# The spacer of the weight stage: first product of V of a later pair in place of the first product of scores and v

## The chip, the cores and the metric

The kernel runs on one core of a Trainium2 chip. The metric is the device time of one execution in microseconds (us). Before the change it is 1761.79 us, the median of three runs (1760.82 to 1763.11). One execution was also recorded by the hardware profiler; its span, from the first to the last instruction, is 1759.4 us. The engines go by these names: PE is TensorE (matrix products), PEld its weight loads, DVE is VectorE, ACT is ScalarE, POOL is GpSimd, SP is SyncE. A "q" behind a name is the engine's instruction queue.

## The reference, cut to what matters

`x` has 64 samples of 256 tokens and 512 features in fp32, `adj` is 256 x 256, and the weights are 512 x 512. Two layers follow each other:

```python
# layer 0
h = relu(layernorm(x))
q, k, v = h @ Wq.T, h @ Wk.T, h @ Wv.T
rel = adj.T * (q @ k.T)
rel = rel / norm(rel, axis=2)          # one norm for each row
x = x + rel @ v
# layer 1
h = relu(layernorm(x))
x = x + (adj @ h) @ weight + bias
```

The samples do not depend on each other. Nothing but the order of the work is at stake here: the change computes the same numbers with the same operations.

## The kernel before, in words

The kernel takes two samples at a time, a **pair**; there are 32 pairs (`NP`). For each pair it computes, in this order: layer norm 0 and its transpose `ht`; `g`, which is `h` times the product of the two weights Wq and Wk, made once at the start (`project_g`, L264); `V = h Wv` (`v_products`, L276); the scores `rel` from `g` and `h` (`scores`, L288), which are then masked, normed, and transposed by blocks (16 small transfers, `placed`, and four transposes on DVE, `turns`, L546); the product of scores and v, added to `x` (called **attend** here, `attend_steps`, L612, adds in L619); layer norm 1; the gather with `adj` (`gather_steps`, L675); and the **weight stage** `mix`, which multiplies by `weight` and adds to `x` (L276 again, adds in L703). Then the pair is written out.

Each of these large products is done by a scheme of Winograd's kind: the operands are cut in 2 x 2 blocks, seven block products take the place of eight, and DVE makes sums of blocks ahead of them. The seven steps use the PSUM tiles `bank_a`, `bank_c`, `bank_b`; after a step, a `take` copies (ACT) or adds (DVE) the tile to its place, while PE goes on with the next. In `project_g`, V and `mix` one of the seven, step 2, is cut once more in the same way ("two levels"): its seven small products go to a tile `bank_d` in four groups, and DVE adds them in small operations (L449, L491). `two_level_steps` (L234) puts the groups between the six large products, which it calls `one`, `five`, `six`, `three`, `seven`, `four`. The last group needs that DVE has already added the third one, so a `spacer`, a product from another part of the work, may be put in front of it:

```python
lambda: run([seven, groups[2]]),
lambda: run([spacer, groups[3]] if spacer else [groups[3]]),
lambda: run([four]),
```

The order of instructions on PE, DVE and ACT is written out by hand: each engine runs its instructions as the program lists them. No planner moves them. The dictionaries in the calls (`{0: ..., 1: ...}`, called `side`) hang DVE and ACT work behind the steps of a product: slot 3 is what is listed after the fourth step and its take. The waits between engines, and which of the eight PSUM buffers a tile gets, are set by the framework.

`steady(i)` (L894) works on several pairs at once, and runs for i = 1 to 28. Its stages are:

1. attend of pair i, interleaved step by step with V of pair i+1 (`attend_and_v`, L623). In its side slots: layer norm 0 of pair i+3 (`totals`, `mean`, `row_squares`, ... on ACT and DVE), the sums for the scores (`gs`), and the last operands of attend itself (`late`)
2. scores of pair i+1
3. `project_g` of pair i+2, with the first part of the gather of pair i as its spacer
4. the rest of the gather of pair i
5. `mix` of pair i. Its spacer is `attends[0]`, the first product of attend of pair i+1. The next pass then leaves this product out (`first_done`)

The operands of attend of pair i+1 are prepared by DVE: `v_steps` make four sums of blocks of V (L133 to L136), `turns` transpose the scores (slot 4 of `mix`), and `rel_steps` make four sums of those (L168 to L171). The first attend product needs the first transposes and a block of V alone; the second needs `v_steps[1]` and `rel_steps[1]`, the third `v_steps[2]` and `rel_steps[2]`. `last_pairs` (L935) finishes the three last pairs.

Of the kernel before, what the change touches and what calls it, by code (L numbers as in the profile page):

```python
# [19 lines left out]
def kernel(  # L20
# [65 lines left out]
    def load(i, queue=nc.sync):  # L86
        X[i] = ring[i % len(ring)]
        queue.dma_start(out=X[i], in_=xs[i])
# [64 lines left out]
    def run(steps):  # L153
        for step in steps:
            step()
# [78 lines left out]
    def two_level_steps(product, take, matmul, add, spacer):  # L234

        one, five, six, three, seven, _, four = winograd_steps(product, take)
        groups = second_level(matmul, add)
        return [  # L240
            lambda: run([one]),
            lambda: run([five]),
            lambda: run([six, groups[0]]),
            lambda: run([three, groups[1]]),
# [4 lines that stand above are left out]
# [125 lines left out]
    def ln0_by_scalar(i):  # L374
        H[i] = work.tile([P, TC, D], F32, tag="hy", name=f"h_{i}")
        return norm_by_scalar(flat(X[i]), H[i])
# [91 lines left out]
    def v_products(i):  # L468
        V[i] = twice.tile([P, NB, NC, D], F32, tag="v", name=f"v_{i}")

        def take(t, k, bank, first):
            dst = V[i][:, :, t, k * HD : (k + 1) * HD]
            src = bank.rearrange("p (b e) -> p b e", b=NB)
            if first:
                nc.scalar.copy(dst, src)  # L475
            else:
                nc.vector.tensor_add(dst, src, dst)

        return product_weights_moving(HL[i], wv_right), take

    def project_v(i, side={}):
        winograd(*v_products(i), side)

    def second_weights_moving(left, right, x):

        def matmul(out, n, start):
            nc.tensor.matmul(out, left[n], right[n], start=start, stop=True, skip_group_check=True)  # L487

        def add(b, k, sums):
            dst = x[:, b, 0, 0:HD] if k is None else x[:, b, 0, ts(k, P)]  # L490
            nc.vector.tensor_add(dst, sums, dst)  # L491

        return matmul, add

    def v_steps_by_two_levels(i):
        products = v_products(i)
        second = second_weights_moving(HL2.pop(i), wv_second, V[i])
        return two_level_steps(*products, *second, None)
# [107 lines left out]
    def attend_steps(i):  # L606

        xt, (left, right) = X[i], R.pop(i)

        def product(bank, n, start):  # L610
            for b in range(NB):
                nc.tensor.matmul(  # L612
                    bank[:, ts(b, HD)], left[n][:, b], right[n][:, b],
                    start=(start and b == 0), stop=True, skip_group_check=True,
                )

        def take(t, k, bank, first):
            dst = xt[:, :, t, ts(k, HD)]
            nc.vector.tensor_add(dst, bank.rearrange("p (b e) -> p b e", b=NB), dst)  # L619

        return winograd_steps(product, take)

    def attend_and_v(i, first_done, steps, side):  # L623


        for at, (step, v_step) in enumerate(zip(steps, v_steps_by_two_levels(i + 1))):
            if at or not first_done:
                step()
            v_step()
            run(side.get(at, ()))  # L630


# [188 lines left out]
    def pairs(exact):  # L821
        with tc.manual_schedule(engines=in_order):
            sums = first_pairs(exact)
            attends, late = attend_steps(1), []
            for i in range(1, NP - 3):
                if i + 4 < NP:
                    load(i + 4)
                sums, attends, late = steady(i, exact, sums, attends, late, first_done=i > 1)
            last_pairs(exact, sums, attends, late)

    def first_pairs(exact):

# [58 lines left out]
        })  # L891
        return sums3

    def steady(i, exact, sums, attends, late, first_done):  # L894

        gs = g_operands(i + 1)
        totals, mean, row_squares, root0, end0, relus0 = ln0_by_scalar(i + 3)  # L900
        stats, root, end, relus, uppers, lowers = ln1(i, exact)
        halves = [stats[b * NC + t] for t in range(NC) for b in range(NB)]
        attend_and_v(i, first_done, attends, {
            0: late[0:3] + totals[0:2], 1: late[3:4] + totals[2:4] + [mean] + sums[0:1],
            2: row_squares[0:2] + sums[1:3], 3: row_squares[2:4] + [root0, end0] + sums[3:4],
            4: relus0[0:2] + gs[0:1], 5: relus0[2:4] + gs[1:3], 6: gs[3:4] + halves[0:1],
        })
        place_blocks(i + 3)
        h_second = second_of_h(i + 2)
        masks, squares, norm_root, inverse, scales, place, turns = scores(i + 1, {  # L910
            0: halves[1:2], 1: halves[2:3], 2: halves[3:4], 3: [root], 4: [end] + relus[0:1],
            5: relus[1:2], 6: uppers[0:2] + h_second,
        })
        turned, sums = transpose_blocks(i + 3)
        y_products, y_steps = gather_steps(i, exact)
        project_g(i + 2, {
            0: masks[0:1] + lowers[0:1] + relus[2:3],
            1: masks[1:2] + lowers[1:2] + relus[3:4],
            2: uppers[2:4] + squares[0:2] + turned[0:2],
            3: lowers[2:3] + squares[2:4] + [norm_root] + turned[2:4],  # L920
            4: lowers[3:4] + [inverse] + scales + [place] + turned[4:5],
            5: turned[5:8],
        }, second=True, spacer=y_products[0])
        v_steps, rel_steps = attend_operands(i + 1)
        run_steps(y_products[1:], {0: v_steps[0:1], 1: v_steps[1:2]})
        run(y_steps[0:2])
        y_second = second_of_y(i)
        attends = attend_steps(i + 1)
        mix(i, {
            0: y_steps[2:3], 1: y_steps[3:4] + y_second[0:2], 2: y_second[2:4],  # L930
            4: turns, 5: rel_steps[0:2],
        }, spacer=attends[0])
        return sums, attends, v_steps[2:3] + rel_steps[2:4] + v_steps[3:4]

    def last_pairs(exact, sums, attends, late):  # L935

        a, b, c = NP - 3, NP - 2, NP - 1
        gs = g_operands(b)
        stats, root, end, relus, uppers, lowers = ln1(a, exact)
        halves = [stats[e * NC + t] for t in range(NC) for e in range(NB)]  # L940
        run(late)
        attend_and_v(a, True, attends, {
            1: sums[0:1], 2: gs[0:2], 3: gs[2:3], 4: gs[3:4], 5: sums[1:2], 6: halves[0:2],
        })
        masks, squares, norm_root, inverse, scales, place, turns = scores(b, {
            0: halves[2:3], 1: halves[3:4] + [root], 2: [end], 3: relus[0:1],
            4: relus[1:2], 5: uppers[0:1], 6: uppers[1:2] + sums[2:4],
        })
        project_g(c, {
            0: masks[0:1] + lowers[0:1] + relus[2:3],  # L950
            1: masks[1:2] + lowers[1:2] + relus[3:4],
            2: uppers[2:4] + squares[0:2],
            3: lowers[2:3] + squares[2:4] + [norm_root],
            4: lowers[3:4] + [inverse] + scales + [place],
        })
        y_steps = gather(a, exact)
        gs = g_operands(c, spare_blocks())
        project_v(c, {
            0: gs[0:1], 1: gs[1:2], 2: gs[2:3] + y_steps[0:1], 3: gs[3:4], 4: y_steps[1:2],
            5: y_steps[2:4], 6: turns,  # L960
        })
        masks, squares, norm_root, inverse, rn, turn_at_once = scores(c, by_matmul=True)
        stats, *parts = ln1(b, exact)
        attend(b, by_slot({n: [stats[n]] for n in range(TC)}, {
            1: masks[0:1], 2: masks[1:2] + squares[0:2], 3: squares[2:4],
        }))
        mix(a, by_slot({0: [norm_root, inverse]}, layer_1(parts)))
        turn_at_once()
        y_steps = gather(b, exact)
        stats, *parts = ln1(c, exact)  # L970
        attend(c, {0: [stats[0], y_steps[0]], 1: [stats[1], y_steps[1]], 2: [stats[2]], 3: [stats[3]]}, rn)
        mix(b, by_slot({0: y_steps[2:3], 1: y_steps[3:4]}, layer_1(parts)))
        y_steps = gather(c, exact)
        run(y_steps[0:2])
        mix(c, {0: y_steps[2:4]})
# [36 lines left out]
```

## Time and profile before

The profile's page gives each engine's busy time and its share of the span; each group of instructions has a row with its busy time, the mean of one instruction, and how long the engine stood idle just before it. The rows for the stages around the change:

| what | line, engine | mean of one | count in all |
|---|---|---|---|
| V product, matmuls (and those of `mix`) | L276 PE | 379 ns | 8 records to a product |
| attend product, matmuls | L612 PE | 379 to 397 ns | 4 records to a product |
| small products of V and `mix` | L487 PE | 274 to 291 ns | 2 records to a product |
| copy of a V product | L475 ACT | 586 ns | 96 from `bank_a` |
| add of a `mix` product | L703 DVE | 691 ns | 128 from `bank_a`, 64 from `bank_c` |
| add of an attend product | L619 DVE | 685 ns | 116 from `bank_a` |
| transposes of scores | L546 DVE | 411 ns | 124 |
| small adds to V and `x` | L491 DVE | 281, 283 ns | 145, 140 of 128 columns |
| sums of V blocks | L133 to L136 DVE | 682 to 692 ns | 29 each |

Matmuls overlap, so the mean of one is longer than the distance from one to the next. In the timeline a row merges equal instructions that follow each other; the distance between the starts of two rows tells what the first of them takes from PE when nothing waits.

Three terms are of use. The **chain of waits** follows the run back from its last instruction, at each step to what released it. A **releaser** is the instruction that an engine was waiting for when it stood idle. A **slot** is a place in a side dictionary.

### The profile page before, as it was taken

What the parts mean: (1) busy time and instruction counts of PE and PEld (TensorE: products, weight loads), DVE (VectorE), ACT (ScalarE), POOL (GpSimd) and SP (SyncE); (2) the same over time, 40 slices, a digit from 0 to 9 for tenths busy, and PEclk for the clock granted to TensorE, in tenths of its full rate; (3) what the DMA queues carried; (4) which work ended last, traced back from release to release, by engine and by line L of the source; (5) the groups of instructions that cost most, each with busy time, mean ns of one, the idle gap of its engine ahead of it and who ended that gap; (6) DMA issues with size and microseconds to landing.
All of it is one profiled execution on the core that took longest, in us unless ns stands there. A gap on an engine that the chain in (4) does not pass through costs nothing.

```text
span 1759.4 us, 27004 instructions
## 1 busy us (share of the span) xinstructions
PE 1711.0 (97%) x9680; PEld 1525.2 (87%) x9680; DVE 1393.6 (79%) x3141; ACT 791.4 (45%) x1835; POOL 192.2 (11%) x167
## 2 busy tenths in 40 slices
PE   9999999999999999999999999999999999999998
PEld 7888988889888898888898888988888988889886
DVE  6778887788877888877888778887778888788765
ACT  3434544445444355444454344554444544445332
POOL 0011110111101111001111011110011110111111
PEclk9999999999999999999999999999999999999999
DMA  7423332323332333323233322333233332322002
GB/s 233 66 50 61 76 81 68 75 38 79 78 76 69 57 64 74 83 65 61 56 78 79 74 71 41 79 74 83 63 60 61 76 81 69 75 37 57 28 13 75
DMA packets 425984, 122.48 MB, mean 70 GB/s; under 512 B 398064, under 2 KB 399344, under 8 KB 425840
## 3 DMA queue, kind: packets, MB, share of 16 engines
q1 hardware_dynamic: 413248, 80.28, 24.4%
q0 software_dynamic: 8432, 32.51, 4.9%
q10 hardware_dynamic: 4160, 7.87, 1.3%
q8 instruction: 79, 1.29, 0.3%
q14 instruction: 65, 0.53, 0.1%
HBM read 38.27 MB, written 33.55 MB: 41 GB/s over the span
## 4 chain that ended last, share of the span: by engine, by line
PE 92%; DVE 4%; SPq 1%; issue 1%; DMA 1%; ACT 0%; DVEq 0%; ACTq 0%
PE bank_a L276 24%; PE bank_c L276 12%; PE bank_a L264 12%; PE py L675 7%; PE bank_a L288 6%; PE bank_c L264 6%; PE bank_a L612 6%; PE bank_d L487 5%; PE bank_c L288 3%; PE bank_c L612 3%; PE bank_d L440 3%; PE bank_b L288 2%; PE bank_b L612 1%; DVE x_ring L703 1%; DVE x_ring L491 1%
## 5 line engine op out<-in xcount | busy, mean ns | idle before, releaser
L475 ACT COPY v<-bank_a 128x512 f32<-128x512 f32 x96 | 56.2, 586 | 582.5 <-PE bank_a L276 582.5
L647 POOL TENSOR_TENSOR x_ring<-x_ring,bias_bc 128x512 f32<-128x512 f32 x128 | 167.4, 1327 | 841.9 <-ACT h2c L319 841.9
L703 DVE TENSOR_TENSOR x_ring<-bank_a,x_ring 128x512 f32<-128x512 f32 x128 | 88.4, 691 | 61.9 <-PE bank_a L276 61.9
L675 PE MATMUL py<-adjt_r,h 128*128 128x256 f32 x1024 | 136.5, 287 | 0.0
L319 ACT ACTIVATE h2c<-x_ring,nb,rs 128x512 f32<-128x512 f32 x128 | 100.6, 810 | 63.8 <-DVE h L655 45.1
L675 PEld LDWEIGHTS py<-adjt_r,h 128*128 128x128 f32 x1024 | 125.3, 189 | 1.6
L276 PE MATMUL bank_a<-w_t,ys 128*128 128x256 f32 x512 | 121.1, 379 | 0.3 <-DVE ys L170 0.3
L264 PE MATMUL bank_a<-hs,m_t 128*128 128x256 f32 x512 | 121.0, 379 | 0.0
L276 PE MATMUL bank_a<-wv_t,hs 128*128 128x256 f32 x512 | 120.9, 379 | 0.0
L276 PEld LDWEIGHTS bank_a<-wv_t,hs 128*128 128x128 f32 x512 | 97.3, 190 | 13.2
L276 PEld LDWEIGHTS bank_a<-w_t,ys 128*128 128x128 f32 x512 | 92.9, 190 | 14.6 <-DVE ys L170 0.7
L264 PEld LDWEIGHTS bank_a<-hs,m_t 128*128 128x128 f32 x512 | 95.1, 190 | 11.8
L715 POOL DMA_DIRECT2D out_dram<-x_ring x31 | 24.0, 773 | 705.2 <-issue 515.3
L307 DVE BATCH_NORM_STATS2 st<-x_ring 128x6 f32<-128x512 f32 x144 | 96.4, 670 | 0.4
L416 DVE STREAM_TRANSPOSE ht<-blocks 128x256 f32<-128x256 f32 x248 | 93.5, 417 | 3.6 <-DMA blocks<-h 3.3
L655 DVE TENSOR_TENSOR h<-h2c,h 128x512 fp32r<-128x512 f32 x128 | 92.3, 723 | 3.0 <-ACT h L651 2.9
L354 ACT ACTIVATE h<-x_ring,nb,rs 128x512 f32<-128x512 f32 x112 | 82.0, 803 | 12.4 <-DVE nb L351 12.4
L619 DVE TENSOR_TENSOR x_ring<-bank_a,x_ring 128x512 f32<-128x512 f32 x116 | 79.5, 685 | 9.9 <-PE bank_a L612 9.9
L679 ACT COPY yt<-py 128x512 f32<-128x512 f32 x128 | 74.4, 581 | 25.6 <-PE py L675 25.6
L536 ACT ACTIVATE rel<-rel,rn 128x256 f32<-128x256 f32 x124 | 52.9, 497 | 68.5 <-DVE rn L533 68.5
L340 ACT ACTIVATE h<-x_ring,sm 128x512 f32<-128x512 f32 x112 | 79.5, 714 | 0.0
L651 ACT CAST h<-h2c 128x512 fp32r<-128x512 f32 x128 | 72.8, 616 | 0.0
(229 smaller groups left out, 4105.0 us busy)
## 6 DMA issues: line engine op xcount, KB each, us to landing
blocks<-h SPq DMA_DIRECT2D x496, 64.0 KB, 2.3
out_dram<-x_ring POOLq DMA_DIRECT2D x31, 1024.0 KB, 4.7
x_ring<-in_x_dram SPq DMA_DIRECT2D x28, 1024.0 KB, 5.2
placed<-rel SPq DMA_DIRECT2D x496, 32.0 KB, 2.0
x_ring<-in_x_dram ACTq DMA_DIRECT2D x4, 1024.0 KB, 5.4
wq_sb<-in_L_gnn_Wq_dram SPq DMA_DIRECT2D x4, 256.0 KB, 5.1
wk_sb<-in_L_gnn_Wk_dram ACTq DMA_DIRECT2D x4, 256.0 KB, 6.2
wv_sb<-in_L_gnn_Wv_dram ACTq DMA_DIRECT2D x1, 1024.0 KB, 5.2
```

The lines of the kernel that those rows point to most:

```text
L264: nc.tensor.matmul(bank[:, e * HT_ : (e + 1) * HT_], right[n][:, d, ts(e, P)], left[n][:, d, :], start=(start and e == 0 and d == 0), stop ...
L276: nc.tensor.matmul(bank[:, b * HD : (b + 1) * HD], left[n][:, d, ts(b, P)], right[n][:, d, :], start=(start and b == 0 and d == 0), stop=( ...
L288: nc.tensor.matmul(bank[:, ts(b, P)], right[n][:, d, ts(b, P)], left[n][:, d, ts(b, P)], start=(start and b == 0 and d == 0), stop=(d == H ...
L307: nc.vector.bn_stats(st[:, c, :], src[:, c, :])
L319: nc.scalar.activation(dst, src[:, c, :], AF.Relu, bias=nb[:, c : c + 1], scale=rs[:, c : c + 1])
L416: nc.vector.transpose(ht[:, d, half].rearrange("p (b n) -> p b n", b=NB), by_half[:, :, half, d])
L487: nc.tensor.matmul(out, left[n], right[n], start=start, stop=True, skip_group_check=True)
L612: nc.tensor.matmul(bank[:, ts(b, HD)], left[n][:, b], right[n][:, b], start=(start and b == 0), stop=True, skip_group_check=True,)
L647: nc.gpsimd.tensor_tensor(xt[:, c, :], xt[:, c, :], bias_bc, ALU.add)
L655: nc.vector.tensor_sub(dst[:, 1, c, :], whole_h[c], dst[:, 0, c, :].bitcast(F32))
L675: nc.tensor.matmul(pm[:, d, :], left[:, b * NC + m, ts(d0 + d, P)], right, start=(n == 0), stop=(n == len(terms) - 1),)
L703: nc.vector.tensor_add(xt[block], bank.rearrange("p (b e) -> p b e", b=NB), xt[block])
```

## The change

The spacer of `mix` becomes the first V product of pair i+2; the first attend product of pair i+1 goes back to the attend stage, directly behind the weight stage. Hence the attend stage now begins with its own first step, and leaves out the first step of V. As the last operands of attend are needed a little earlier now, they are no longer made in the attend stage (`late`), but in slots 3 and 6 of `mix`. The freed side slots of the attend stage are evened out. The purpose is that the spacer should be work whose operands are long there.

```diff
-    def attend_and_v(i, first_done, steps, side):
-        for at, (step, v_step) in enumerate(zip(steps, v_steps_by_two_levels(i + 1))):
+    def attend_and_v(i, first_done, v_products, side):
+        for at, (step, v_step) in enumerate(zip(attend_steps(i), v_products)):
+            step()
             if at or not first_done:
-                step()
-            v_step()
+                v_step()
             run(side.get(at, ()))
...
-            attends, late = attend_steps(1), []
+            v_products = v_steps_by_two_levels(2)
...
-    def steady(i, exact, sums, attends, late, first_done):
+    def steady(i, exact, sums, v_products, first_done):
...
-        attend_and_v(i, first_done, attends, {
-            0: late[0:3] + totals[0:2], 1: late[3:4] + totals[2:4] + [mean] + sums[0:1],
-            2: row_squares[0:2] + sums[1:3], 3: row_squares[2:4] + [root0, end0] + sums[3:4],
+        attend_and_v(i, first_done, v_products, {
+            0: totals[0:2] + sums[0:1], 1: totals[2:4] + [mean] + sums[1:2],
+            2: row_squares[0:2] + sums[2:3], 3: row_squares[2:4] + [root0, end0] + sums[3:4],
             4: relus0[0:2] + gs[0:1], 5: relus0[2:4] + gs[1:3], 6: gs[3:4] + halves[0:1],
         })
...
-        attends = attend_steps(i + 1)
+        v_products = v_steps_by_two_levels(i + 2)
         mix(i, {
             0: y_steps[2:3], 1: y_steps[3:4] + y_second[0:2], 2: y_second[2:4],
-            4: turns, 5: rel_steps[0:2],
-        }, spacer=attends[0])
-        return sums, attends, v_steps[2:3] + rel_steps[2:4] + v_steps[3:4]
+            3: v_steps[2:4], 4: turns, 5: rel_steps[0:2], 6: rel_steps[2:4],
+        }, spacer=v_products[0])
+        return sums, v_products
...
-    def last_pairs(exact, sums, attends, late):
+    def last_pairs(exact, sums, v_products):
...
-        run(late)
-        attend_and_v(a, True, attends, {
+        attend_and_v(a, True, v_products, {
```

More of the change, by code (lines that the diff above doesn't have):

```diff
@@ L827, in pairs @@
                     load(i + 4)
-                sums, attends, late = steady(i, exact, sums, attends, late, first_done=i > 1)
-            last_pairs(exact, sums, attends, late)
+                sums, v_products = steady(i, exact, sums, v_products, first_done=i > 1)
+            last_pairs(exact, sums, v_products)
     def first_pairs(exact):
```

## The prediction

> **What bounds the kernel now.** First the page: which engine is full, and at what clock.
>
> ```profile
> span 1759.4 us, 27004 instructions
> PE 1711.0 (97%) x9680; PEld 1525.2 (87%) x9680; DVE 1393.6 (79%) x3141; ACT 791.4 (45%) x1835; POOL 192.2 (11%) x167
> ...
> PEclk9999999999999999999999999999999999999999
> ```
>
> TensorE has work almost always, at full clock (the mean granted clock is 0.999), and the chain that ended last runs 92% over it. So only two things can shorten the run: less TensorE work, or fewer TensorE waits. The list of waits of PE names one that repeats; the other matmul waits of the whole run are under 6 us together.
>
> ```profile
> PE bank_a L612 <- DVE turned L546: 36.8, 28, 1.4
> ```
>
> 28 waits, one for each `steady` pair, 36.8/28 = 1.31 us each and 1.4 at most: every pair loses the same. The timeline of PE around one of them (columns: start, length, engine, line, operation, count, idle before it):
>
> ```profile
> 820.23 1.89 PE L276 MATMUL bank_a<-w_t,ys 128*128 128x256 f32 x8
> 821.96 0.38 PE L487 MATMUL bank_d<-w_t,ys 128*128 128x128 f32 x2
> 822.18 0.39 PE L487 MATMUL bank_d<-w_sb,yt 128*128 128x128 f32 x2
> 823.88 1.10 PE L612 MATMUL bank_a<-v,turned 128*128 128x256 f32 x4 [1.31 <-DVE turned L546]
> 824.82 0.39 PE L487 MATMUL bank_d<-w_t,yt 128*128 128x128 f32 x2
> 825.04 1.89 PE L276 MATMUL bank_a<-w_t,yt 128*128 128x256 f32 x8
> 826.77 1.89 PE L276 MATMUL bank_a<-wvt_sb,ht 128*128 128x256 f32 x8
> 828.50 1.03 PE L612 MATMUL bank_c<-v,turned 128*128 128x256 f32 x4
> 829.36 1.89 PE L276 MATMUL bank_c<-wvt_sb,ht 128*128 128x256 f32 x8
> ```
>
> Read it by starts. A full product of weights or V takes 1.73 (825.04 to 826.77), an attend product 0.86 (828.50 to 829.36), a pair of 128-wide matmuls 0.22 (821.96 to 822.18). After the third row PE could go on at 822.18 + 0.22 = 822.40. The spacer, the first product of scores and v (`attends[0]`, L612), starts at 823.88: 1.48 late. It then takes 0.94 to the next start in place of 0.86. The loss is 1.48 + 0.08 = **1.56 us per pair**, of which the wait shows 1.31, since the printed ends lie later than the point at which the next matmul could start. What it waited for is in DVE's timeline:
>
> ```profile
> 819.99 0.69 DVE L703 TENSOR_TENSOR x_ring<-bank_c,x_ring 128x512 f32<-128x512 f32 x1 [0.72 <-PE bank_c L276]
> 820.60 0.28 DVE L491 TENSOR_TENSOR x_ring<-bank_d,x_ring 128x128 f32<-128x128 f32 x1
> 822.16 0.69 DVE L703 TENSOR_TENSOR x_ring<-bank_a,x_ring 128x512 f32<-128x512 f32 x1 [1.28 <-PE bank_a L276]
> 822.77 0.61 DVE L491 TENSOR_TENSOR x_ring<-bank_d,x_ring 128x128 f32<-128x128 f32 x2
> 823.30 1.41 DVE L546 STREAM_TRANSPOSE turned<-placed 128x256 f32<-128x256 f32 x4
> ```
>
> DVE idles 1.28 until the fifth big product (`seven`) ends, adds it, adds the two small sums, and only then transposes the scores (`turns`, L546). The spacer needs the first of these transposes. Thus a product meant to fill a pause waits for the very queue that made the pause.
>
> **What the Trainium skill says.** "Perfetto Trace Analysis", section "Tensor Engine Instruction (MATMUL, LD_WEIGHTS)": ends of matmuls are estimated from their size. The trace agrees: rows of 1.89 follow each other every 1.73; hence my counting by starts. "TensorE: Matmul & The Clock Gate", "Step-by-step: what each phase is for": matmuls stay in program order, only weight loads are pulled ahead. The trace agrees: `group_4` (824.82) and `four` (825.04) need no transpose and still stand behind the spacer. "PSUM — Partial Sum Buffer", "Specifications (TRN2)": 8 banks of 512 fp32 values; each `bank_*` or `py` tile fills one. No row of the trace shows which bank a tile has, so this feeds a rival.
>
> **The change, part by part.**
>
> 1. *Spacer.* `attends[0]` leaves the slot, `v_products[0]` of pair i+2 enters: 8 matmuls, 1.73 us in all. Its operands are `ht` and `wvt_sb`. `project_g(i+2)` has already read this `ht` over 10 us before, so it waits for no operand. Work between 822.40 and the later V product is the same set in another order, so no PE work is added: 0.
>
> 2. *The new order on PE*, from 822.40 with the steps above: V product to 824.13, `group_4` to 824.35, `four` to 826.08, attend product 1 to 826.94, attend product 2 to 827.81, then V product 2, which before started at 829.36. 829.36 - 827.81 = 1.55, if nothing waits.
>
> 3. *DVE's queue.* `v_steps[2:4]` come from the attend stage to slot 3 (L135 and L136, 0.68 each, starts 0.6 apart). They enter behind the L491 of 820.60 and end at about 822.2, where DVE had idled to 822.16: cost 0 to 0.15. Then the add of `seven` to 822.9, two small adds to 823.4, four transposes to 824.75, the add of `group_4` to 825.05, `rel_steps[0:2]` (0.42 each) to 825.9, the add of `four` at 826.2 to 826.9, `rel_steps[2:4]` to 827.7, the add of attend product 1 to 828.4.
>
> 4. *What PE needs from it.* `group_4` at 824.13 needs the small adds (823.4): 0.7 to spare. Attend product 1 at 826.08 needs the transposes (824.75): 1.3. Product 2 at 826.94 needs `rel_steps[1]` and `v_steps[1]` (825.9): 1.0. Product 3 at 829.54 needs the add of product 1 (828.4): 1.1. None waits; the thinnest is 0.7, before `group_4`.
>
> 5. *ACT.* The V product is taken by an ACT copy (L475, 0.58) in the weight stage. In this pair ACT had idled 16.01 us ahead of that very copy: 0.
>
> 6. *Attend and V stage.* It loses four DVE operations (2 x 0.68 + 2 x 0.42 = 2.2 us) and 1.73 of PE, and gains one attend product (0.86 PE, 0.69 DVE): DVE has less to do there. `totals[2:4]` still stand behind the second V copy and `mean` behind them, so they keep their distance to PE. The transfers that place the blocks start at the end of the last attend product, in the same order as before: 0. Work of `scores`, `project_g` and the gather is untouched.
>
> 7. *Ends.* The first pass has no spacer behind it in either order, and `last_pairs` takes the spacer of the last of the 28 passes. The wait that vanishes occurs 28 times.
>
> Sum: 28 x 1.55 = 43.4; 1761.8 - 43.4 = **1718.4 us**, some 2.5% less. The lower bound of the gain from the waits alone is 36.8 (1725.0).
>
> **Rivals.**
>
> *A, the wait reappears smaller.* DVE is the other busy engine (43.7 busy of 54.0 us of a pair). If its queue is 1.1 us later than I draw it, `group_4` or an attend product waits 0.4 us: 28 x 0.4 = 11.2, **1729.6**. For it: two more operations of 0.68 in front of the transposes. Against: DVE idled 1.28 exactly there, and the only other regular wait of TensorE for DVE, that of V's own `group_4` (weight loads for L491: 11.3 us, 28 times), is 0.4 and has no V product in front of it, only an attend product of 0.86.
>
> *B, a PSUM bank comes late at the start of the weight stage.* The spacer's set of tiles, asked for before `mix`, has four banks now against three, `mix` has four: all eight. If `mix`'s first product gets the bank of the last gather tile, it waits for that tile's ACT copy, which ends at 812.69, where the product now starts at 811.91: 0.8 per pair, 22.4, **1740.8**. Against: eleven tiles over the three sets share eight banks in either order, and the trace has no PE wait of this kind.
>
> *C, slower.* If also attend product 1 gets the bank of `four`, it waits until DVE has added it. The add of `four` started at 826.97 and ended 0.69 later, 0.9 after that product's last matmul had given way (826.77). 0.8 + 0.9 = 1.7 of new waits against 1.55 saved: 28 x 0.15 = +4, **1766**. For: attend tiles are now first used directly behind `four`. Against: the V tiles stood in that place before and started at once at 826.77.
>
> **How the numbers follow.** The forecast has 0.71 (1716 to 1722: the loss is the same in every pair, and the saving is 1.48 to 1.63 according to how the starts are rounded). A and smaller mixtures have 0.17 (1722 to 1737), B 0.05, no net change 0.02, C 0.05. Below 1716 I leave 0.02, from the forecast's share. The range 1716 to 1731 holds 0.69 of the forecast and some 0.11 of A, so 0.8. Faster: 0.71 + 0.17 + 0.05 = 0.93; within 0.2%: 0.02; slower: 0.05.
>
> **What would show it.** Right: no wait of PE for `turned`; the V product (bank_a from `wvt_sb`, `ht`) starts 0.22 after the last L487 of the third group; L612 rows for bank_a and bank_c stand one behind the other after `four`; the spacing of pairs falls from 53.94 (823.88 to 877.82) to 52.4; PE at about 99% of its span. A shows as a wait of L487 for L491, or of L612 for L169 or L619; B as a wait of L276 (`yt`) for the copy L679; C as a wait of the first L612 for L703. The prediction is wrong if one of these is over 0.15 us per pair, or if DVE's `mean` (L337) falls later against PE and pushes adds into the V groups.

## The result, and the profile after

The changed kernel takes **1718.93 us** (median of 4 runs, 1717.26 to 1719.96), against 1762.22 us for the kernel before in the runs beside it. The ratio is 0.9754, with a 95% interval of 0.9737 to 0.9771: 43.3 us less. The prediction said 1718.4.

The page of the kernel after, its first lines and the granted clock:

```profile
span 1715.2 us, 27061 instructions
PE 1704.2 (99%) x9680; PEld 1523.6 (89%) x9680; DVE 1386.5 (81%) x3141; ACT 794.5 (46%) x1835; POOL 192.2 (11%) x167
...
PEclk9999999999999999999999999999999999999999
```

The number of PE instructions and the clock are the same; the span fell by 44.2, while PE's busy time fell by 7 only. So what went was idle time, and the 7 us were no work either: per pair the loss read by starts (1.56) exceeds the printed wait (1.31) by 0.25, and 28 x 0.25 = 7.0. Of this 0.25, 0.17 is the printed end of the row ahead of the wait (822.18 + 0.39 = 822.57), which lies later than the point at which PE could go on (822.40), and 0.08 is the slower start after the wait. PE's list of waits in the kernel after (line, releaser, total, count, longest) begins so:

```profile
PE pf L758 <- DVE low_max L756: 1.3, 1, 1.3
PE pz L743 <- POOL warm L105: 1.0, 1, 1.0
PE bank_a L276 <- DMA wk_sb<-in_L_gnn_Wk_dram: 1.0, 1, 1.0
```

The row of 28 waits for `turned` is gone. What is left at the head belongs to the start of the run, each once. PE's timeline at the place of the change, kernel after:

```profile
802.50 0.39 PE L487 MATMUL bank_d<-w_sb,yt 128*128 128x128 f32 x2
802.73 1.89 PE L276 MATMUL bank_a<-wvt_sb,ht 128*128 128x256 f32 x8
804.45 0.39 PE L487 MATMUL bank_d<-w_t,yt 128*128 128x128 f32 x2
804.67 1.89 PE L276 MATMUL bank_a<-w_t,yt 128*128 128x256 f32 x8
806.40 1.03 PE L612 MATMUL bank_a<-v,turned 128*128 128x256 f32 x4
807.27 1.03 PE L612 MATMUL bank_c<-v,turned 128*128 128x256 f32 x4
808.13 1.89 PE L276 MATMUL bank_c<-wvt_sb,ht 128*128 128x256 f32 x8
809.86 1.03 PE L612 MATMUL bank_a<-blocks,rel 128*128 128x256 f32 x4
```

No row carries an idle time. From the moment PE is free after the third group (802.73) to the second V product (808.13) it takes 5.40 us; before it was 829.36 - 822.40 = 6.96. The difference is 1.56, the loss that was read off the trace of before. DVE's timeline of the same stretch, kernel after:

```profile
800.92 0.28 DVE L491 TENSOR_TENSOR x_ring<-bank_d,x_ring 128x128 f32<-128x128 f32 x1
801.11 0.68 DVE L135 TENSOR_TENSOR blocks<-v 128x512 f32<-128x512 f32 x1
801.83 0.69 DVE L136 TENSOR_TENSOR blocks<-v,blocks 128x512 f32<-128x512 f32 x1
802.48 0.69 DVE L703 TENSOR_TENSOR x_ring<-bank_a,x_ring 128x512 f32<-128x512 f32 x1
803.09 0.61 DVE L491 TENSOR_TENSOR x_ring<-bank_d,x_ring 128x128 f32<-128x128 f32 x2
803.62 1.42 DVE L546 STREAM_TRANSPOSE turned<-placed 128x256 f32<-128x256 f32 x4
804.96 0.25 DVE L491 TENSOR_TENSOR x_ring<-bank_d,x_ring 128x128 f32<-128x128 f32 x1
805.13 0.41 DVE L168 TENSOR_TENSOR rel<-turned 128x256 f32<-128x256 f32 x1
805.57 0.43 DVE L169 TENSOR_TENSOR turned<-turned 128x256 f32<-128x256 f32 x1
```

The two moved sums (L135, L136) fill the pause of 1.28 us that stood in front of L703 before. DVE does the transposes no earlier against PE than before: 1.12 us after the start of the last L487 row (803.62 - 802.50; before 823.30 - 822.18). Only nobody waits for them now; their reader starts at 806.40.

### The profile page after: what moved, and what is told of

The parts are those of the page before. It is cut to its first block, busy times and chain, and to the rows that moved or that the text cites. A ratio compares the mean times of both kernels' runs of the same rounds, so it can differ in the third digit from the quotient of the medians.

```text
span 1715.2 us, 27061 instructions
## 1 busy us (share of the span) xinstructions
PE 1704.2 (99%) x9680; PEld 1523.6 (89%) x9680; DVE 1386.5 (81%) x3141; ACT 794.5 (46%) x1835; POOL 192.2 (11%) x167
## 4 chain that ended last, share of the span: by engine, by line
PE 97%; DVE 2%; DMA 0%; ACT 0%; issue 0%; ACTq 0%; DVEq 0%
PE bank_a L276 26%; PE bank_c L276 13%; PE bank_a L264 13%; PE py L675 7%; PE bank_a L288 7%; PE bank_c L264 6%; PE bank_d L487 6%; PE bank_a L612 6%; PE bank_c L288 3%; PE bank_c L612 3%; PE bank_d L440 3%; PE bank_b L288 2%; PE bank_b L612 1%; PE bank_b L276 1%; PE pu L577 1%; DVE st L307 0%
## 5 line engine op out<-in xcount | busy, mean ns | idle before, releaser
L276 PE MATMUL bank_a<-w_t,ys 128*128 128x256 f32 x512 | 121.1, 379 | 0.3 <-DVE ys L170 0.3
L276 PE MATMUL bank_a<-wv_t,hs 128*128 128x256 f32 x512 | 120.9, 379 | 0.0
L703 DVE TENSOR_TENSOR x_ring<-bank_a,x_ring 128x512 f32<-128x512 f32 x128 | 88.5, 691 | 35.1 <-PE bank_a L276 35.1
L276 PEld LDWEIGHTS bank_a<-wv_t,hs 128*128 128x128 f32 x512 | 97.3, 190 | 13.2
L276 PEld LDWEIGHTS bank_a<-w_t,ys 128*128 128x128 f32 x512 | 92.9, 190 | 14.6 <-DVE ys L170 0.7
L264 PEld LDWEIGHTS bank_a<-hs,m_t 128*128 128x128 f32 x512 | 95.1, 190 | 11.8
L334 ACT ACTIVATE h<-x_ring 128x512 f32<-128x512 f32 x112 | 69.5, 623 | 40.5 <-PE bank_a L276 40.5
L679 ACT COPY yt<-py 128x512 f32<-128x512 f32 x128 | 74.5, 582 | 26.1 <-PE py L675 26.1
L619 DVE TENSOR_TENSOR x_ring<-bank_a,x_ring 128x512 f32<-128x512 f32 x116 | 79.3, 683 | 1.0 <-PE bank_a L612 1.0
```

The costliest lines, as they stand in the source:

```text
L264: nc.tensor.matmul(bank[:, e * HT_ : (e + 1) * HT_], right[n][:, d, ts(e, P)], left[n][:, d, :], start=(start and e == 0 and d == 0), stop ...
L276: nc.tensor.matmul(bank[:, b * HD : (b + 1) * HD], left[n][:, d, ts(b, P)], right[n][:, d, :], start=(start and b == 0 and d == 0), stop=( ...
L703: nc.vector.tensor_add(xt[block], bank.rearrange("p (b e) -> p b e", b=NB), xt[block])
```

## The experiments

In what follows, group 3 and group 4 are the last two of the four groups of small products. Two theories were told apart first. **Theory 1**: the gain is the wait of the spacer for the transposes. **Theory 2**: it is the better spread of DVE's work over the slots, which the change also contains.

**The slots alone.** The kernel before, with the side slots of the kernel after (those of the attend stage too, which the cut leaves out):

```diff
...
-            4: turns, 5: rel_steps[0:2],
+            3: v_steps[2:4], 4: turns, 5: rel_steps[0:2], 6: rel_steps[2:4],
         }, spacer=attends[0])
-        return sums, attends, v_steps[2:3] + rel_steps[2:4] + v_steps[3:4]
+        return sums, attends, []
```

> The kernel before with the side slots of the kernel after (no late operands, v_steps[2:4] and rel_steps[2:4] in mix), but with the first attend product still as the spacer. Theory 1 (the gain is the spacer's wait for the transposes that vanished): the wait stays, and the transposes come 0 to 0.15 us later behind the two moved sums: 1762 to 1766 us, a wait of L612 for turned of 1.3 to 1.5 us, 28 times. Theory 2 (the gain comes from DVE's work being spread better): about 1719 us.

Measured: 1761.87 us, ratio to before 1.0001 (0.9992 to 1.0009). PE's waits in this run:

```profile
PE bank_a L612 <- DVE turned L546: 36.7, 28, 1.4
```

The wait is as long as before (36.8), and the time did not move. Theory 2 falls.

**The spacer alone.** The kernel after, with the late operands where they were before:

```diff
...
-            3: v_steps[2:4], 4: turns, 5: rel_steps[0:2], 6: rel_steps[2:4],
+            4: turns, 5: rel_steps[0:2],
         }, spacer=v_products[0])
-        return sums, v_products
+        return sums, v_products, v_steps[2:3] + rel_steps[2:4] + v_steps[3:4]
```

> The kernel after with the late operands kept in the attend stage, in the slots of the kernel before; the spacer is the V product. Theory 1: 1717 to 1723 us; the third attend product needs rel_steps[2], which would end some 0.5 us before that product can start, so no wait of TensorE, or one below 0.15 us per pair (4 us). Theory 2: about 1762 us. A third reading (the moved slots are needed so that the new order does not wait for its own operands): the third attend product waits for L170 or L171 by 0.3 us or more per pair, 1727 us or more.

Measured: 1718.91 us, ratio 0.9755 (0.9739 to 0.9771). It is the whole gain. So the spacer's place is what counts, and moving the four DVE operations, which the change does as well, is not needed for it.

**No spacer at all.** Is it enough that nothing waits for the transposes, or must a product cover DVE's adds?

```diff
...
-        }, spacer=v_products[0])
+        }, spacer=None)
...
```

with the first V product back in the attend stage.

> The kernel after without any spacer in mix: the V product goes back to the attend stage. Theory 1 with its second half (the V product also covers DVE's adds of the third group): group 4 waits until L491 has ended, in the trace of after at 803.70 where TensorE is free at 802.73: 1.0 us and 0.1 for the restart, 28 x 1.1 = 31, so 1750 us, with a wait of L487 for L491. Rival (the only fault of before was the transposes; without them in the way no cover is needed): within 5 us of 1719.

Measured: 1752.56 us, ratio 0.9946 (0.9929 to 0.9962). PE's waits, and the timeline of PE and of DVE's adds of group 3 in this run:

```profile
PE bank_d L487 <- DVE x_ring L491: 26.8, 28, 1.0
```

```profile
871.96 0.39 PE L487 MATMUL bank_d<-w_sb,yt 128*128 128x128 f32 x2
872.55 0.61 DVE L491 TENSOR_TENSOR x_ring<-bank_d,x_ring 128x128 f32<-128x128 f32 x2
873.30 0.46 PE L487 MATMUL bank_d<-w_t,yt 128*128 128x128 f32 x2 [0.96 <-DVE x_ring L491]
873.60 1.89 PE L276 MATMUL bank_a<-w_t,yt 128*128 128x256 f32 x8
```

Group 4 waits for DVE's adds of group 3. It could have started at 871.96 + 0.22 = 872.18 and started at 873.30, 1.12 late; its own row then took 0.30 to the next start in place of 0.22. 28 x (1.12 + 0.08) = 33.6, and the run is 33.6 us slower than after. DVE's last add ended at 872.55 + 0.61 = 873.16 in this pair, so PE followed it by 0.14.

**Half the spacer.** The V product as the spacer, but only four of its eight records, as long as an attend product (0.86); the rest goes to the attend stage:

```diff
...
+            steps[0] = second_half
+            steps.insert(0, lambda: product(bank, n, start, (0,)))
...
```

> The kernel after with only the first half of the V product (4 of its 8 matmul records, 0.86 us, as long as an attend product) as the spacer; the second half and the ACT copy go back to the attend stage, behind the first attend product. Operands ready as in after, cover as short as in before: it tells readiness from length. Theory 1: TensorE is free 0.86 after the third group (803.59 in the trace of after), L491 ends at 803.70 and group 4 started 0.14 behind it in the run without a spacer: 0.25 and 0.08 for the restart, 28 x 0.33 = 9, 1728 us. If only readiness counts: 1719. If the length is nearly all (the cover of 0.86 is too little): 1740 or more.

Measured: 1726.88 us, ratio 0.9803 (0.9787 to 0.982). PE's timeline in this run (its lines are shifted: L286 is L276, L497 is L487):

```profile
912.35 0.39 PE L497 MATMUL bank_d<-w_sb,yt 128*128 128x128 f32 x2
912.57 1.03 PE L286 MATMUL bank_a<-wvt_sb,ht 128*128 128x256 f32 x4
913.70 0.46 PE L497 MATMUL bank_d<-w_t,yt 128*128 128x128 f32 x2
913.99 1.89 PE L286 MATMUL bank_a<-w_t,yt 128*128 128x256 f32 x8
```

No idle time is printed, since the printed length of 1.03 covers most of the gap (912.57 + 1.03 = 913.60); the starts show it: 912.57 + 0.86 = 913.43, group 4 at 913.70, 0.27 late, and 0.07 for the restart. 28 x 0.34 = 9.5 against the 8.0 measured. So of the 43 us, some 35 come when a product of the same length has its operands ready, and some 8 more from the greater length.

**More DVE work in front.** How thin was the 0.7 us to spare at group 4? The sum `v_steps[3]` is done twice, or three times:

```diff
-            3: v_steps[2:4], 4: turns, ...
+            3: v_steps[2:4] + v_steps[3:4], 4: turns, ...
```

> The kernel after with one DVE operation more in slot 3 of mix (v_steps[3] is done twice, 0.68 us, the same result again). It tests the spare time of 0.7 us that I gave to group 4. The operation delays the adds by 0.6 to 0.72: they end at 804.3 to 804.45 in the trace of after, where group 4 starts at 804.45. Theory 1: 0 to 0.15 us per pair, 1719 to 1723 us. Rival (DVE's queue bounds the kernel now, every operation of DVE is paid): 28 x 0.65 = 18, 1737 us.

> The kernel after with two DVE operations more in slot 3 of mix (v_steps[3] is done three times). The adds end 1.2 to 1.45 later, at 804.9 to 805.15, group 4 then waits 0.5 to 0.8 and restarts: 28 x 0.5 to 0.8 = 14 to 22, so 1733 to 1741 us, with a wait of L487 for L491, 28 times. If the spare time were much larger than 0.7: no change (1719). If every operation of DVE is paid: 1755.

Measured: 1723.12 us (ratio 0.9788, 0.9771 to 0.9804) with one more, 1741.70 us (0.9894, 0.9878 to 0.9911) with two. The first operation is nearly free: 4.2 us or 0.15 per pair for 0.7 us of DVE time. The second costs 18.6 us, 0.66 per pair, nearly all of its length. PE's waits, PE's timeline and DVE's timeline in the run with two more:

```profile
PE bank_d L487 <- ACT v L475: 17.6, 28, 0.6
```

```profile
866.77 1.89 PE L276 MATMUL bank_a<-wvt_sb,ht 128*128 128x256 f32 x8
869.29 0.46 PE L487 MATMUL bank_d<-w_t,yt 128*128 128x128 f32 x2 [0.63 <-ACT v L475]
```

```profile
865.87 2.15 DVE L136 TENSOR_TENSOR blocks<-v,blocks 128x512 f32<-128x512 f32 x3
867.93 0.68 DVE L703 TENSOR_TENSOR x_ring<-bank_a,x_ring 128x512 f32<-128x512 f32 x1
868.54 0.61 DVE L491 TENSOR_TENSOR x_ring<-bank_d,x_ring 128x128 f32<-128x128 f32 x2
```

The releaser named here is a copy on ACT, and it is the wrong one. Group 4 reads and writes nothing that the copy of V touches, and in the kernel after it starts at 804.45, before that copy has begun (804.65). The adds L491 end at 868.54 + 0.61 = 869.15, and group 4 follows 0.14 later, the same distance as in the run without a spacer; it is 0.14 to 0.15 in all 28 pairs of both runs. The copy (868.70, 0.58 long) only happened to end closest to the start.

**The transposes earlier.** The other way to serve the spacer of before: let DVE do what it needs where DVE idles.

```diff
-            4: turns, 5: rel_steps[0:2],
+            3: turns[0:2], 4: turns[2:4], 5: rel_steps[0:2],
         }, spacer=attends[0])
```

> The kernel before with the first two transposes one slot earlier (slot 3), which are all that the spacer needs; nothing else is changed. If the transposes could run where DVE idles (820.9 to 822.2 in the trace of before), the spacer would start at once and only group 4 would wait, gain 1.3 x 28 = 36: 1726 us. My theory: the 16 transfers that they read are issued from 809.52 to 820.46 and take about 2.0 us to land, so the transposes wait until 822.5, end at about 823.2, and push the adds of seven and of the third group to 824.4; four then starts about 0.3 us earlier than before: gain 8, 1754 us. DVE then shows a wait of turned L546 for the transfer, 28 times.

Measured: 1743.49 us, ratio 0.9892 (0.9876 to 0.9909): between the two numbers, and 10.5 below my own. DVE's waits, and PE's, in this run:

```profile
DVE turned L546 <- DMA placed<-rel: 31.8, 28, 2.2
```

```profile
PE bank_d L487 <- DVE x_ring L491: 7.8, 25, 0.4
PE bank_a L612 <- DVE turned L546: 5.3, 8, 1.1
```

One of the pairs, with the row of the 16 issues in the queue of SP and the transposes behind them:

```profile
856.92 10.40 SPq L543 DMA_DIRECT2D placed<-rel  x16
868.86 0.77 DVE L546 STREAM_TRANSPOSE turned<-placed 128x256 f32<-128x256 f32 x2 [0.84 <-DMA placed<-rel]
```

The mechanism was right: the transposes wait for the transfers, 28 times. The size was off: I had a wait of 1.6, and the mean is 31.8/28 = 1.14. I had counted the 2.0 us to landing from the end of the row of issues. In the pair above the issues end at 856.92 + 10.40 = 867.32 and DVE goes on at 868.86, 1.54 later; the last issue began at 866.7, 2.2 earlier. From pair to pair the wait varies from 0.63 to 2.15, for the most part because the issuing itself does: it takes 10.4 us in many pairs and up to 11.8 (11.57 in the pair with the wait of 2.15), while DVE goes on 1.3 to 1.7 after its end in 27 of the 28 pairs, and 2.7 in one. The spacer still waits in 8 pairs only, and group 4 waits 7.8/25 = 0.3 us in nearly all. So a wait that varies by 1.5 us stands on the path of this version; in the changed kernel DVE's list has no wait for these transfers.

**A version faster than both.** If a wait of 0.2 us in front of a small group is real, more ready work in front of it must remove it. Three such places were found. In V's own second level (kernel after, PE's timeline) the sixth attend product is followed by group 4:

```profile
871.44 1.03 PE L612 MATMUL bank_b<-v,turned 128*128 128x256 f32 x4
872.48 0.49 PE L487 MATMUL bank_d<-wv_t,ht 128*128 128x128 f32 x2
872.80 1.03 PE L612 MATMUL bank_a<-blocks,turned 128*128 128x256 f32 x4
```

It starts 1.04 after the product in place of 0.86, and takes 0.32 in place of 0.22. The adds of the third group stand just ahead of it; in another pair of the same trace group 4 starts at 820.00, and DVE's row is

```profile
819.33 0.61 DVE L491 TENSOR_TENSOR v<-bank_d,v 128x128 f32<-128x128 f32 x2
```

These adds end at 819.94, so here PE follows by 0.06. The edit puts the seventh attend product in front of it as well:

```diff
...
+            if at == 5:
+                steps[6]()
...
```

> The kernel after, in which group 4 of V stands behind the last two attend products in place of one. In the trace of after the sixth attend product starts at 818.97 and could be followed at 819.83, but group 4 starts at 820.00 and four's successor 0.32 later in place of 0.22: 0.27 us per pair. With 1.73 us of work in front it does not wait: 28 x 0.27 = 7.6, 1711 us. Rival (that gap is not the wait for L491 but the restart of small products): no change, 1719 us.

Measured: 1711.41 us, ratio 0.972 (0.9704 to 0.9736). PE's timeline in this run:

```profile
921.02 1.03 PE L612 MATMUL bank_b<-v,turned 128*128 128x256 f32 x4
921.88 1.03 PE L612 MATMUL bank_a<-blocks,turned 128*128 128x256 f32 x4
922.75 0.38 PE L487 MATMUL bank_d<-wv_t,ht 128*128 128x128 f32 x2
922.97 1.89 PE L276 MATMUL bank_a<-wv_t,ht 128*128 128x256 f32 x8
```

Every row now follows at its own pace: 0.86, 0.87, 0.22. The same was done in `project_g`, with two gather products as the spacer:

```diff
-        }, second=True, spacer=y_products[0])
+        }, second=True, spacer=lambda: run(y_products[0:2]))
         v_steps, rel_steps = attend_operands(i + 1)
-        run_steps(y_products[1:], {0: v_steps[0:1], 1: v_steps[1:2]})
+        run_steps(y_products[2:], {0: v_steps[0:2]})
```

With it, `v_steps[0:2]` go into one slot.

> The kernel after with two gather products in front of group 4 of project_g in place of one. In the trace of after the first gather row and group 4 lose 0.12 + 0.10 us per pair: 28 x 0.22 = 6, 1713 us. Rival (ACT's copies of the gather products come in the way of the copy of four, so that bank or y comes late): 1719 or more, with a new wait of L276 or L264 for ACT.

Measured: 1710.94 us, ratio 0.9717 (0.9701 to 0.9734). Group 4 of `project_g` takes 0.23 to the next start in this run (890.51 to 890.74), against 0.33 in the kernel after (840.17 to 840.50), and PE's list has no new wait. And the first two operands of the second level of y were made one slot earlier:

```diff
-            0: y_steps[2:3], 1: y_steps[3:4] + y_second[0:2], 2: y_second[2:4],
+            0: y_steps[2:3] + y_second[0:2], 1: y_steps[3:4], 2: y_second[2:4],
```

> The kernel after with L168 and L169 of the second level of y in slot 0 of mix in place of slot 1. The first group of mix loses 0.07 + 0.11 us per pair in after: 28 x 0.18 = 5, 1714 us. Rival (the gap is not a wait for L169): 1719. The rest of the gain of the kernel with all three edits over that with group 4 of V alone (1711.4 to 1701.2, thus 10.2 us) is to be the sum of this edit and of the gather edit.

Measured: 1713.43 us, ratio 0.9727 (0.9711 to 0.9743). The two rows of the first group take 0.22 each in this run (848.92, 849.14, 849.36), against 0.29 and 0.33 in the kernel after (850.24, 850.53, 850.86). With all three edits together:

> The kernel after with three small edits of the same kind: group 4 of V behind two attend products, group 4 of project_g behind two gather products in place of one (the trace of after shows 0.12 + 0.10 lost there per pair), and the first two operands of the second level of y (L168, L169) one slot earlier in mix (0.07 + 0.11 lost per pair in front of the first group). If all are waits that work in front of them can cover: 28 x (0.27 + 0.22 + 0.18) = 19, 1700 us. If only the first one counts: 1711. If new waits come up: 1719 or more.

Measured: **1701.18 us** (4 runs, 1700.51 to 1701.32), ratio to before 0.9662 (0.9646 to 0.9678), the fastest of all. Against the ratio of after, 0.9754, the three edits take off 0.0034, 0.0037 and 0.0027, in sum 0.0098, and together 0.0092: they add up within their intervals. A pair takes 51.85 us in this version, 52.44 after the change, and 53.98 before (the mean over the 28 passes, from the first L288 row of a pass to that of the next).

## Why the prediction was right

1. *The size of the loss* was read by starts, 1.56 per pair, not from the printed wait of 1.31. The sum of printed waits would have given 1725; the measured 1718.93 lies 0.5 from the sum by starts. Over all 28 passes, from the first L288 row of the first to the one behind the last, the trace of before takes 1653.77 - 142.28 = 1511.49 and that of after 1609.72 - 141.29 = 1468.43: 43.06 less, 1.54 per pair.
2. *The new order on PE* came as drawn: the rows of after are spaced 1.72, 0.22, 1.73, 0.87, 0.86.
3. *DVE's queue*: the two moved sums were put at 0 to 0.15. L703 stands 0.02 ahead of the last L487 row before and after (822.16 against 822.18, 802.48 against 802.50): 0.
4. *The spare times* at group 4 and at the first three attend products were put at 0.7, 1.3, 1.0 and 1.1. The trace of after shows 0.75, 1.36, 1.27 and 1.18 (804.45 less the end of the adds, 803.70; 806.40 less 805.04; 807.27 less 806.00; 809.86 less 808.68, the end of the add L619). Of the first, 0.14 is the distance at which PE follows DVE, so 0.6 was free; the two runs with more DVE work bracket it.
5. *ACT* had idled 11.29 us in front of the moved copy (16.01 before): 0, as said.
6. *`mean`* kept its distance: 3.78 us behind the start of the second V product, before (833.14 - 829.36) and after (811.91 - 808.13).
7. *The rivals.* A did not occur, but its mechanism is real: with two more operations in DVE's queue it appears, at 0.8 us per pair. B and C did not occur: after has no wait of the first product of `mix` for L679, nor of L612 for L703. That no product waited for a bank is seen; which bank a tile has is not.

One thing the prediction did not separate: it read the whole loss as a wait for operands that were not ready, and used the length of the V product in its sum (0.7 to spare at group 4) without saying what a ready product of 0.86 would leave. The half spacer shows that about 8 of the 43 us need the greater length as well, since DVE's adds of group 3 end 1.0 us after PE comes free and an attend product covers 0.86.

## What to carry to other kernels

A product that is to fill a pause must itself wait for nothing that stands behind the pause in the same queue, and it must be longer than the rest of that queue: here the adds end 1.0 us after PE comes free, and group 4 follows 0.14 later. Read the loss by the starts of rows and compare each distance with the same row where nothing waits; gaps of 0.2 us hide inside printed lengths, and three of them were worth 18 us. Where a wait is put down to an engine that the instruction has no operand from, look for the last writer of its operands.

## What the runs showed of the hardware

Where group 4 of `mix` had to wait, it started 0.14 to 0.15 us after DVE's last add had ended (873.30 behind 873.16, 869.29 behind 869.15, 912.29 behind 912.14 with one operation more), and its pair of small matmuls then took 0.30 in place of 0.22. That distance is no constant of every wait: group 4 of V started 0.06 after its last add (820.00 behind 819.94) and took 0.32. In the kernel after, the profile books this second wait to TensorE's weight load (PEld, 11.8 us, 29 times) and none to its matmul; whether that makes the difference is not shown.

The 16 transfers of a pair took one queue 10.4 to 11.8 us to issue in the run with the early transposes, and DVE could go on 1.3 to 1.7 us after the last issue had ended (2.7 in one of 28 pairs). With PE busy at 99% of its span the granted clock of the recorded run was 0.999, as it was before the change at 97%.
